# Two attribute maps in one product, and a shorter first piece of each layer's input, in a three-layer graph network on one Trainium2 core

## The chip, the cores and the metric

The kernel runs on one core of one Trainium2 chip. The metric is the device time of one execution in microseconds (us). The text calls the engines by the names that the profile uses: PE multiplies matrices (PEld is its loading of the stationary operand), DVE is the vector engine, ACT the scalar engine, POOL the general one, and SP issues transfers.

## The reference, cut to what matters

There are N = 6250 nodes with D = 64 features and E = 200000 edges with EC = 16 attributes; `src` and `dst` give the ends of an edge. A first network of two layers (SAGE) comes first and does not concern us. The second network has three message layers, each over the edges and one self loop for each node (whose attributes are all ones):

```
def _mp_layer(x, src_f, dst_f, ea_f, W, b):
    m = concatenate([x[dst_f], x[src_f], ea_f], axis=1) @ W.T + b
    return relu(segment_sum(m, dst_f, num_segments=n))

h = _mp_layer(x, ..., W0, b0);  h = relu(_batchnorm(h, g0, be0))
h = _mp_layer(h, ..., W1, b1);  h = relu(_batchnorm(h, g1, be1))
h = _mp_layer(h, ..., W2, b2)
x = layernorm(x + h)
```

Since a sum over edges and a linear map commute, a message layer is three sums per node: the adjacency matrix times the mapped features of the sources, the node's own mapped features times its in-degree, and the node's summed attributes (with its in-degree, for the bias) times the attribute part of W. The batch normalization takes mean and variance over all nodes, so no input of the next layer exists before the last node of a layer is done.

## The kernel before, in words

The nodes are padded to NB = 49 blocks of P = 128, in NT = 13 tiles of up to four blocks (TW = 512 nodes; the last tile has one block). A first half of the kernel builds the adjacency matrix as counts in 8 bits, `adj8`, tile by tile of destinations; every later layer loads a tile's 49 x 512 columns (`load_adj`) and multiplies. Features go in as three bf16 parts of 64 columns each, which together carry an fp32 value: `split` (L626 to L633) writes them into `parts`.

`ext` is a table of 128 rows by 6272 nodes. Its rows 0 to 47 are the three bf16 parts of the summed attributes, rows 48 to 63 are zero, and every row from 64 up holds the in-degree. `extT[n]` is the stationary side for layer n: the attribute columns of W three times, the bias at row 64, and zeros elsewhere.

`aggregate` (L640) makes the products of one or two tiles. `product` (L650) multiplies one 128 x 128 block of the adjacency with one block of `parts` (192 columns); 49 such products, one for each source block b, fill one destination block's sum in PSUM. `term` (L657) adds the node's attribute part to the same sum: one product of `ext` with `extT[n]` for each destination block, in layers 1 and 2 (`terms`). For the first two tiles of a layer (`src_first`), the loop over b is outside and the eight destination blocks inside, so that PE can start as soon as the first source block exists; `feed(b)` makes more source blocks on the way. For the other eleven tiles a destination block is the outer loop.

`next_input` (L1103) makes a piece of a layer's input from the layer before: ACT applies the normalization and the relu (L1107), PE multiplies with `maps` (L1110), `split` makes the three parts, and DVE makes the node's own share `own` (L1113, L1114). A piece has four blocks. `feed` calls it for piece 0 and piece 1 at b = 0 and for one piece more at every fourth block.

`first_message` (layer 0) sums the parts, transposes (L700, ACT copies the result to `mx`, L702), and makes two products into one PSUM tile `lin`: `catT` with the features (L1131) and `extT[0]` with `ext` (L1132). ACT takes the relu into `hr` (L1133). `message_layer` (layers 1 and 2) sums the parts (L675), adds `own` (L1142), and in layer 1 transposes (L1146) and takes the relu from PSUM into `hr` (L1147). `statistics` (L1118) collects a tile's mean and variance. At the end of a layer, L1188 to L1194 turn these into the scale and bias `sc`.

The order of instructions on each engine is made when the program is built, by a list scheduler that works from the program order and its own cost estimates. `pin` marks an instruction that is not to move against other marked ones. Pools decide how far an engine can run ahead: two `agg` tiles, two `u` tiles, one `tr` and one `lin` tile of PSUM, two buffers of `h1` (the input of L1110).

Of the kernel before, what the change touches and what calls it, by code (L numbers as in the profile page):

```python
# [11 lines left out]
F32 = mybir.dt.float32  # L12
# [4 lines left out]
AF = mybir.ActivationFunctionType  # L17
ALU = mybir.AluOpType
# [4 lines left out]
P = 128  # L23
# [453 lines left out]
def gnn_kernel(ctx: ExitStack, tc: tile.TileContext, x, src, dst, ea, W_l1, b_l1, W_r1, W_l2, b_l2, W_r2,  # L477
# [10 lines left out]
    nc = tc.nc  # L488
# [63 lines left out]
    with ExitStack() as fast:  # L552
# [22 lines left out]
        for n in range(3):  # L575


            if n == 0:
                catT.append(const.tile([2 * D, D], F32, name="catT"))
            else:  # L580
                maps.append(const.tile([D, 2 * D], F32, name=f"maps{n}"))
            extT.append(const.tile([P, D], F32, name=f"extT{n}"))
            nc.vector.memset(extT[n], 0.0)

        def load_weights():
            def transposed(to, of, at=0):
                p = psm.tile([P, P], F32, name="tr")
                k, m = of.shape
                nc.tensor.transpose(p[:m, :k], of, ident[:k, :k])
                nc.scalar.copy(to, p[:m, :k])  # L590

            nc.sync.dma_start(bl1, b_l1.rearrange("(p o) -> p o", o=1))
            nc.sync.dma_start(bl2, b_l2.rearrange("(o d) -> o d", o=1).to_broadcast([P, D]))
            for to, w in ((w1s[:D, :], W_l1), (w1s[D:, :], W_r1), (w2s[:, :D], W_l2), (w2s[:, D:], W_r2)):
                t = spare(w.shape[1])[: w.shape[0], :]
                nc.sync.dma_start(t, w)
                transposed(to, t)
            for n, (w, b) in enumerate(((W0, b0), (W1, b1), (W2, b2))):
                t = spare(2 * D + 3 * EC)[:D, :]
                for r in range(3):  # L600
                    nc.sync.dma_start(t[:, 2 * D + r * EC: 2 * D + (r + 1) * EC], w[:, 2 * D:])
                nc.sync.dma_start(t[:, : 2 * D], w[:, : 2 * D])
                nc.sync.dma_start(extT[n][D: D + 1, :], b.rearrange("(o d) -> o d", o=1))
                if n == 0:
                    transposed(catT[0], t[:, : 2 * D])
                else:
                    transposed(maps[n - 1][:, D:], t[:, : D])
                    transposed(maps[n - 1][:, : D], t[:, D: 2 * D])
                transposed(extT[n][: 3 * EC, :], t[:, 2 * D:])
            for n, (g, be) in enumerate(((g0, be0), (g1, be1))):  # L610
                gam.append(const.tile([D, 1], F32, name=f"gam{n}"))
                bet.append(const.tile([D, 1], F32, name=f"bet{n}"))
                nc.sync.dma_start(gam[n], g.rearrange("(p o) -> p o", o=1))
                nc.sync.dma_start(bet[n], be.rearrange("(p o) -> p o", o=1))
# [25 lines left out]
        def aggregate(psa, pt, tiles, n, src_first=False, feed=None, terms=None, sources=range(NB)):  # L640

            views = [view(a, j) for a, j in tiles]
            sums = [psa.tile([P, 4, TW // 2], F32, name="agg") for _ in tiles]
            blocks = [(k, i) for k, (_, j) in enumerate(tiles) for i in range(tw(j) // P)]

            def product(k, i, b):

                nc.tensor.matmul(sums[k][:, i, :n], views[k][:, b, i * P: (i + 1) * P], pt[:, b, :n],  # L650
                                 start=(b == sources[0] and terms is None and not (src_first and i % 2)), stop=(b == sources[-1]),
                                 skip_group_check=src_first or terms is not None)

            def term(k, i):
                if terms is not None:
                    at = tiles[k][1] * TW + i * P
                    nc.tensor.matmul(sums[k][:, i, : terms[1].shape[1]], terms[0][:, at: at + P], terms[1],  # L657
                                     start=not (src_first and i % 2), stop=False, skip_group_check=True)

            if src_first:  # L660
                for k, i in blocks:
                    term(k, i)
                for b in sources:
                    feed(b)
                    for k, i in blocks:
                        product(k, i, b)
            else:
                for k, i in blocks:
                    term(k, i)
                    for b in range(NB):  # L670
                        product(k, i, b)
            return sums
# [61 lines left out]
        with ExitStack() as bld:  # L734
# [315 lines left out]
            hot = bld.enter_context(tc.tile_pool(name="ahot", bufs=2))  # L1050
            lhss = [ew.tile([P, EAG, P], BF16, name=f"lhs{k}", bufs=1) for k in range(2)]
            for lhs in lhss:
                nc.gpsimd.memset(lhs[:, :, 3 * EC: D], 0.0)
                nc.gpsimd.memset(lhs[:, :, D:], 1.0)
            selfl = ew.tile([P, 1], F32, name="selfl", bufs=1)
            nc.vector.memset(selfl, 0.0)
            nc.vector.memset(selfl[:EC, :], 1.0)
            nc.vector.memset(selfl[D:, :], 1.0)


            per = -(-NSUB // NT)
# [32 lines left out]

        mp = fast.enter_context(tc.tile_pool(name="fmp", bufs=1))
        hr = mp.tile([D, NPAD], F32, name="hr")
        own = mp.tile([P, NB, D], F32, name="own")
        ok_s = mp.tile([1, 1], I32, name="ok_s")
        psu = fast.enter_context(tc.tile_pool(name="fpsu", bufs=2, space=PSUM))
        nc.sync.dma_start(ok_s, ok_d)  # L1100
        nc.vector.tensor_single_scalar(inv, cnt, 1.0, ALU.add)

        def next_input(n, b, sc, pt):  # L1103

            nb, s = min(4, NB - b), slice(b * P, min(b + 4, NB) * P)
            y = work.tile([D, TW], F32, name="h1")
            nc.scalar.activation(y[:, : nb * P], hr[:, s], AF.Relu, bias=sc[:, 1:2], scale=sc[:, 0:1])  # L1107
            u = psu.tile([P, 4, P], F32, name="u")
            for i in range(nb):
                nc.tensor.matmul(u[:, i, :], y[:, i * P: (i + 1) * P], maps[n - 1], start=True, stop=True)  # L1110
            split(pt[:, b: b + nb, : 3 * D], u[:, :nb, :D], nb)
            o = own[:, b: b + nb, :]
            nc.vector.tensor_mul(o, u[:, :nb, D:], inv[:, b: b + nb].unsqueeze(2).to_broadcast([P, nb, D]))  # L1113
            nc.vector.tensor_add(o, o, u[:, :nb, :D])  # L1114
# [5 lines left out]
        def first_message(j, ps, stats):  # L1120

            w, s = tw(j), slice(j * TW, j * TW + tw(j))
            nb, bs = w // P, j * TW // P
            h = res[:, bs: bs + nb, :]
            nd = work.tile([P, 4, P], F32, name="nd")
            nc.gpsimd.tensor_tensor(nd[:, :nb, :D], h, inv[:, bs: bs + nb].unsqueeze(2).to_broadcast([P, nb, D]), ALU.mult)  # L1126
            add_parts(nd[:, :nb, D:], ps, nb)
            nc.vector.tensor_add(nd[:, :nb, D:], nd[:, :nb, D:], h)
            both = transposed_tile(nd, nb)
            pm = psm.tile([P, TW], F32, name="lin")  # L1130
            nc.tensor.matmul(pm[:D, :w], catT[0], both[:, :w], start=True, stop=False)  # L1131
            nc.tensor.matmul(pm[:D, :w], extT[0], ext[:, s], start=False, stop=True)  # L1132
            nc.scalar.activation(hr[:, s], pm[:D, :w], AF.Relu)  # L1133
            statistics(j, stats)

        def message_layer(n, j, ps, stats):
# [6 lines left out]
            if n < 2:  # L1143
                t = psm.tile([P, 4, P], F32, name="tr")
                for i in range(nb):
                    nc.tensor.transpose(t[:D, i, :], v[:, i, :], ident)  # L1146
                nc.scalar.activation(hr[:, s], t[:D, :nb, :].rearrange("f i p -> f (i p)"), AF.Relu)  # L1147
                statistics(j, stats)
                return
            nc.vector.scalar_tensor_tensor(v[:, :nb, :], v[:, :nb, :], 0.0, res[:, bs: bs + nb, :], ALU.max, ALU.add)  # L1150
# [8 lines left out]
        sc = None  # L1159
        for n in range(3):  # L1160
            pt = parts[n % 2]
            terms = (ext, extT[n]) if n else None
            stats = work.tile([D, NT, nc.vector.BN_STATS_DIM], F32, name="stats") if n < 2 else None
            first = [(load_adj(j), j) for j in range(2)]

            def feed(b):
                if n and b % 4 == 0:
                    if b == 0:
                        next_input(n, 0, sc, pt)
                    if b + 4 < NB:  # L1170
                        next_input(n, b + 4, sc, pt)

            def message(j, ps):
                if n == 0:
# [11 lines left out]
                break  # L1186
            mv = work.tile([D, nc.vector.BN_AGGR_DIM], F32, name="mv")
            nc.vector.bn_aggr(mv, stats.rearrange("p j s -> p (j s)"))  # L1188
            sc = work.tile([D, 2], F32, name="sc")
            nc.scalar.activation(sc[:, 0:1], mv[:, 1:2], AF.Sqrt, bias=eps_t[:D])  # L1190
            nc.vector.reciprocal(sc[:, 0:1], sc[:, 0:1])
            nc.vector.tensor_mul(sc[:, 0:1], sc[:, 0:1], gam[n])
            nc.vector.tensor_mul(sc[:, 1:2], mv[:, 0:1], sc[:, 0:1])
            nc.vector.tensor_sub(sc[:, 1:2], bet[n], sc[:, 1:2])  # L1194
        ok_r = nc.values_load(ok_s[0:1, 0:1], min_val=0, max_val=1)

    with tc.If(ok_r == 0):
# [32 lines left out]
```

## Time and profile before

| | |
|---|---|
| median of 3 runs | 1657.76 us (1656.78 to 1659.83) |
| profiled execution: its own time | 1656.98 us |
| its span, first to last instruction | 1655.2 us |
| mean granted PE clock in it | 0.964 |
| build and first network, with the attribute sums (0 to 945 us of the span) | PE busy 810 us, DVE 767 us, ACT 511 us |
| message layer 0 (945 to 1170) | PE busy 220.7 us, DVE 31.1 us, ACT 13.8 us |
| message layer 1 (1170 to 1411.8) | PE busy 236.5 us, DVE 48.9 us, ACT 26.1 us |
| message layer 2 (1411.8 to the end) | PE busy 229.4 us, DVE 73.1 us, ACT 27.4 us |

The stages were cut at the ends of the layers' last adjacency products. The profile gives the busy time of an engine, what ended its idle times, and the chain of work that ended last; "issue" in that chain is time for which the profile shows no cause.

### The profile page before, as it was taken

How to read it: one execution, taken by the hardware profiler on the slowest of the kernel's cores; microseconds unless marked ns; L12 is line 12 of the kernel's file. 1: busy time of each engine (PE TensorE's matmuls, PEld its weight loads, DVE VectorE, ACT ScalarE, POOL GpSimd, SP SyncE). 2: the span in 40 equal slices, each digit the busy share in tenths (PEclk: the TensorE clock that was granted, in tenths of full speed). 3: DMA queues.
4: the chain of work that ended last, by engine and by line, in shares of the span. 5: the costliest groups of instructions: out<-in, count | busy, mean ns of one | idle time of the engine just before them, and what ended most of it. 6: DMA issues, size and time to landing. Idle time of an engine off the chain costs nothing.

```text
span 1655.2 us, 38577 instructions
## 1 busy us (share of the span) xinstructions
PE 1496.9 (90%) x17135; PEld 1379.9 (83%) x17135; DVE 920.0 (56%) x1581; ACT 578.4 (35%) x1088; POOL 117.0 (7%) x72
## 2 busy tenths in 40 slices
PE   1586789899998989999999999999999999999997
PEld 0475668788887779889999888888899999899997
DVE  2999999998898733897888610001340100442122
ACT  1625466776885721454455300000220000310000
POOL 2024200360001010000000000000000000000000
PEclk9697899999999999999999999999899999899999
DMA  5021332032130373344534444442324542345450
GB/s 163 11 107 55 110 96 85 12 154 83 80 157 2 150 287 159 137 150 183 200 133 142 172 165 179 187 173 99 156 117 197 197 194 99 157 178 227 164 186 10
DMA packets 43811, 228.10 MB, mean 138 GB/s; under 512 B 22978, under 2 KB 30210, under 8 KB 35826
## 3 DMA queue, kind: packets, MB, share of 16 engines
q1 hardware_dynamic: 37058, 139.54, 22.4%
q10 hardware_dynamic: 4496, 79.48, 12.2%
q0 software_dynamic: 2080, 6.52, 1.3%
q8 instruction: 136, 2.23, 0.5%
q14 instruction: 41, 0.34, 0.1%
HBM read 183.76 MB, written 41.75 MB: 136 GB/s over the span
## 4 chain that ended last, share of the span: by engine, by line
PE 62%; DVE 21%; ACT 7%; issue 5%; DMA 3%; ACTq 0%; POOL 0%; DVEq 0%; POOLq 0%
PE agg L650 47%; DVE lo L620 7%; PE pair L958 6%; DVE rhs L620 4%; ACT a L965 4%; PE u L1110 2%; PE bank L1025 2%; DVE e L1016 1%; PE agg L657 1%; DVE e L1018 1%; DMA e<-in_edge_attr_dram 1%; DVE nd L675 1%; PE tr L700 1%; PE lin L1131 1%; DMA a<-adj 1%
## 5 line engine op out<-in xcount | busy, mean ns | idle before, releaser
L650 PE MATMUL agg<-parts,a 128*128 128x192 bf16 (+1 forms) x12005 | 1089.8, 246 | 5.6 <-DVE nd L675 1.8
L650 PEld LDWEIGHTS <-a 128*128 128x128 fp8e3 x12005 | 1008.3, 98 | 23.6 <-issue 12.1
L965 ACT ACTIVATE a<-pair 128x784 fp8e3<-128x784 f32 (+3 forms) x355 | 292.3, 890 | 122.8 <-PE pair L958 121.2
L958 PE MATMUL pair<-rhs,lo 128*128 128x147 bf16 (+5 forms) x2569 | 266.2, 244 | 64.0 <-DVE lo L620 30.3
L958 PEld LDWEIGHTS <-lo 128*128 128x128 bf16 x2569 | 196.2, 104 | 119.4 <-issue 52.1
L620 DVE TENSOR_TENSOR rhs<-iota,k 128x1960 bf16<-128x1960 f16 (+15 forms) x240 | 238.9, 1015 | 13.6 <-ACT k L905 11.3
L620 DVE TENSOR_TENSOR lo<-iota,k 128x2048 bf16<-128x2048 f16 x161 | 194.5, 1215 | 0.0
L675 DVE TENSOR_REDUCE z<-agg 128x256 f32<-128x768 f32 (+1 forms) x39 | 35.3, 910 | 282.7 <-PE agg L650 282.4
L620 DVE TENSOR_TENSOR lo<-iota,e_d 128x2048 bf16<-128x2048 f16 (+11 forms) x132 | 130.7, 1010 | 20.6 <-PE bank L1025 19.8
L1025 PE MATMUL bank<-lo,lhs 128*128 128x128 bf16 x1701 | 107.5, 219 | 17.4 <-ACT lhs L1019 12.1
L1025 PEld LDWEIGHTS <-lhs 128*128 128x128 bf16 x1701 | 98.4, 98 | 28.6 <-ACT lhs L1019 19.4
L675 DVE TENSOR_REDUCE nd<-agg 128x256 f32<-128x768 f32 (+1 forms) x26 | 23.4, 904 | 116.0 <-PE agg L650 116.0
L886 POOL DMA_INDIRECT rows<-cmb_d,start_i x21 | 64.8, 3084 | 207.4 <-ACT key L897 167.0
L1118 DVE BATCH_NORM_STATS2 stats<-hr 64x6 f32<-64x512 f32 (+1 forms) x26 | 17.0, 653 | 101.7 <-ACT hr L1133 80.4
L702 ACT COPY mx<-tr 128x512 f32<-128x512 f32 (+1 forms) x26 | 14.6, 562 | 166.9 <-PE tr L700 166.8
L691 ACT ACTIVATE sp_r<-z 128x256 f32<-128x256 f32 (+1 forms) x26 | 10.5, 403 | 171.4 <-DVE z L690 171.4
L1147 ACT ACTIVATE hr<-tr 64x512 f32<-64x512 f32 (+1 forms) x13 | 7.4, 566 | 179.9 <-PE tr L1146 179.9
L1015 ACT CAST lhs<-e 128x512 bf16<-128x512 f32 (+21 forms) x72 | 36.1, 502 | 59.6 <-PE bank L1025 44.6
L1126 POOL TENSOR_TENSOR nd<-res,inv 128x256 f32<-128x256 f32 (+1 forms) x13 | 7.6, 589 | 550.5 <-DVE ln_s L688 339.2
L1019 ACT CAST lhs<-e 128x512 bf16<-128x512 f32 (+21 forms) x72 | 36.4, 505 | 23.1 <-DVE e L1018 22.6
L1016 DVE TENSOR_TENSOR e<-e,lhs 128x512 f32<-128x512 f32 (+21 forms) x72 | 39.4, 550 | 8.9 <-ACT lhs L1015 8.8
L1017 ACT CAST lhs<-e 128x512 bf16<-128x512 f32 (+21 forms) x72 | 36.3, 504 | 22.2 <-DVE e L1016 21.0
(140 smaller groups left out, 819.6 us busy)
## 6 DMA issues: line engine op xcount, KB each, us to landing
a<-adj SPq DMA_DIRECT2D x24, 3136.0 KB, 12.4
a<-adj ACTq DMA_DIRECT2D x24, 3136.0 KB, 11.5
adj<-a SPq DMA_DIRECT2D x12, 3136.0 KB, 9.6
e<-in_edge_attr_dram SPq DMA_DIRECT2D x25, 256.0 KB, 2.7
a<-adj SPq DMA_DIRECT2D x4, 784.0 KB, 4.2
out_dram<-z SPq DMA_DIRECT2D x12, 128.0 KB, 6.5
a<-first_edges ACTq DMA_DIRECT2D x1, 1216.0 KB
e<-in_edge_attr_dram SPq DMA_DIRECT2D x7, 152.0 KB, 3.3
```

Of the source, the lines that this page charges most:

```text
L620: nc.vector.tensor_tensor(to.rearrange("p g (h two) -> p g h two", two=2), iota[:, :n].rearrange("p (h two) -> p h two", two=2).unsqueeze( ...
L650: nc.tensor.matmul(sums[k][:, i, :n], views[k][:, b, i * P: (i + 1) * P], pt[:, b, :n], start=(b == sources[0] and terms is None and not ( ...
L675: nc.vector.tensor_reduce(to, ps[:, :nb, : 3 * D].rearrange("p b (r d) -> p b d r", r=3), AX.X, ALU.add)
L886: pin(nc.gpsimd.indirect_dma_start(out=rows, out_offset=None, in_=cmb_d[:, :], in_offset=bass.IndirectOffsetOnAxis(ap=start_i[:, t: t + 1] ...
L958: nc.tensor.matmul(pair[:, bank % 2, col: col + wc], lo_hot(t, c), rhs[:, i, :wc], start=first, stop=last)
L965: nc.scalar.activation(av[:, :, o: o + 2 * nd].rearrange("p h (two d) -> p h two d", two=2), pair[:, :, : nd * NB].rearrange("p two (d h) ...
L1015: nc.scalar.copy(lhs[:, :g, 0:EC], r)
L1016: nc.vector.tensor_sub(r, r, lhs[:, :g, 0:EC])
L1017: nc.scalar.copy(lhs[:, :g, EC:2 * EC], r)
L1019: nc.scalar.copy(lhs[:, :g, 2 * EC:3 * EC], r)
L1025: nc.tensor.matmul(ps[:, :P], lhs[:, q, :], oh[:, q % HOT, :], start=(c == 0 and q == 0), stop=(i == last_b[b] and q == g - 1))
L1110: nc.tensor.matmul(u[:, i, :], y[:, i * P: (i + 1) * P], maps[n - 1], start=True, stop=True)
```

## The change

Layer 1's attribute part is taken out of its sums. Instead the product that makes layer 0's attribute part makes layer 1's at the same time: `extT[0]` and `extT[1]` lie side by side in one 128-column stationary operand, `ext01`, and the upper 64 rows of the result are layer 1's share for these nodes. ACT copies them to `e1`, which is the upper half of `ext` itself, whose rows are not needed for these nodes after that. In layer 1, DVE adds `e1` to the transposed sums and ACT takes the relu in place. So that layer 2 finds all that it needs in the lower half of `ext`, the in-degree now begins at row 48, and the bias with it. In layer 0 the `ext` product comes ahead of the `catT` product in program order.

A layer's input now begins with a piece of one block and a piece of three; then come pieces of four as before, and the last of one. Layer 2's `term` products of the first two tiles stand behind the first two pieces in program order, no longer ahead of them, and these and the products of `next_input` are pinned. In the chain from statistics to `sc`, the mean's sign is turned first, and one operation with two steps takes the place of a multiplication and a subtraction.

```diff
-            extT.append(const.tile([P, D], F32, name=f"extT{n}"))
+            if n == 0:
+                ext01 = const.tile([P, 2 * D], F32, name="ext01")
+            extT.append(ext01[:, n * D: (n + 1) * D] if n < 2 else const.tile([P, D], F32, name="extT2"))
...
-                nc.sync.dma_start(extT[n][D: D + 1, :], b.rearrange("(o d) -> o d", o=1))
+                nc.sync.dma_start(extT[n][3 * EC: 3 * EC + 1, :], b.rearrange("(o d) -> o d", o=1))
...
             def term(k, i):
...
+                    if src_first:
+                        pin(first)
             if src_first:
-                for k, i in blocks:
-                    term(k, i)
                 for b in sources:
                     feed(b)
+                    if b == sources[0]:
+                        for k, i in blocks:
+                            term(k, i)
...
-                nc.gpsimd.memset(lhs[:, :, 3 * EC: D], 0.0)
-                nc.gpsimd.memset(lhs[:, :, D:], 1.0)
+                nc.gpsimd.memset(lhs[:, :, 3 * EC:], 1.0)
...
+        e1 = ext[D:, :]
...
-        def next_input(n, b, sc, pt):
+        def next_input(n, b, end, sc, pt):
-            nb, s = min(4, NB - b), slice(b * P, min(b + 4, NB) * P)
+            nb, s = end - b, slice(b * P, end * P)
...
-                nc.tensor.matmul(u[:, i, :], y[:, i * P: (i + 1) * P], maps[n - 1], start=True, stop=True)
+                pin(nc.tensor.matmul(u[:, i, :], y[:, i * P: (i + 1) * P], maps[n - 1], start=True, stop=True))
...
-            nc.tensor.matmul(pm[:D, :w], catT[0], both[:, :w], start=True, stop=False)
-            nc.tensor.matmul(pm[:D, :w], extT[0], ext[:, s], start=False, stop=True)
+            nc.tensor.matmul(pm[:, :w], ext01, ext[:, s], start=True, stop=False, skip_group_check=True)
+            nc.tensor.matmul(pm[:D, :w], catT[0], both[:, :w], start=False, stop=True, skip_group_check=True)
             nc.scalar.activation(hr[:, s], pm[:D, :w], AF.Relu)
+            nc.scalar.copy(e1[:, s], pm[D:, :w])
...
-                nc.scalar.activation(hr[:, s], t[:D, :nb, :].rearrange("f i p -> f (i p)"), AF.Relu)
+                nc.vector.tensor_add(hr[:, s], t[:D, :nb, :].rearrange("f i p -> f (i p)"), e1[:, s])
+                nc.scalar.activation(hr[:, s], hr[:, s], AF.Relu)
...
-            terms = (ext, extT[n]) if n else None
+            terms = (ext[:D, :], extT[n][:D, :]) if n == 2 else None
...
             def feed(b):
-                if n and b % 4 == 0:
-                    if b == 0:
-                        next_input(n, 0, sc, pt)
-                    if b + 4 < NB:
-                        next_input(n, b + 4, sc, pt)
+                ends = [1] + list(range(4, NB, 4)) + [NB]
+                if n and b == 0:
+                    next_input(n, 0, ends[0], sc, pt)
+                if n and b in [0] + ends[:-1]:
+                    q = ([0] + ends).index(b)
+                    if q + 1 < len(ends):
+                        next_input(n, ends[q], ends[q + 1], sc, pt)
...
+            nc.vector.tensor_single_scalar(mv[:, 0:1], mv[:, 0:1], -1.0, ALU.mult)
...
-            nc.vector.tensor_mul(sc[:, 1:2], mv[:, 0:1], sc[:, 0:1])
-            nc.vector.tensor_sub(sc[:, 1:2], bet[n], sc[:, 1:2])
+            nc.vector.scalar_tensor_tensor(sc[:, 1:2], sc[:, 0:1], mv[:, 0:1], bet[n], ALU.mult, ALU.add)
```

More of the change, by code (lines that the diff above doesn't have):

```diff
@@ L656, in term @@
                     at = tiles[k][1] * TW + i * P
-                    nc.tensor.matmul(sums[k][:, i, : terms[1].shape[1]], terms[0][:, at: at + P], terms[1],
-                                     start=not (src_first and i % 2), stop=False, skip_group_check=True)
+                    first = nc.tensor.matmul(sums[k][:, i, : terms[1].shape[1]], terms[0][:, at: at + P], terms[1],
+                                             start=not (src_first and i % 2), stop=False, skip_group_check=True)
+                    if src_first:
+                        pin(first)
             if src_first:
-                for k, i in blocks:
-                    term(k, i)
                 for b in sources:
                     feed(b)
+                    if b == sources[0]:
+                        for k, i in blocks:
+                            term(k, i)
                     for k, i in blocks:
@@ L1052, in gnn_kernel @@
             for lhs in lhss:
-                nc.gpsimd.memset(lhs[:, :, 3 * EC: D], 0.0)
-                nc.gpsimd.memset(lhs[:, :, D:], 1.0)
+                nc.gpsimd.memset(lhs[:, :, 3 * EC:], 1.0)
             selfl = ew.tile([P, 1], F32, name="selfl", bufs=1)
-            nc.vector.memset(selfl, 0.0)
+            nc.vector.memset(selfl, 1.0)
+            nc.vector.memset(selfl[:32, :], 0.0)
+            nc.vector.memset(selfl[32: 3 * EC, :], 0.0)
             nc.vector.memset(selfl[:EC, :], 1.0)
-            nc.vector.memset(selfl[D:, :], 1.0)
             per = -(-NSUB // NT)
```

## The prediction, made before the changed kernel ran

> **What bounds the kernel now.** I first read the page's shares: PE is busy for 1496.9 of 1655.2 us. The chain that ended last says where that matters. In the message layers it runs through PE almost without a break, so there a product removed is time won. This is the chain in the middle of layer 1 (start, duration, what):
>
> ```profile
> 1248.37 1.32 PE agg L650 x16
> 1249.69 0.08 issue
> 1249.78 0.60 PE tr L1146 x4
> 1250.37 2.72 PE agg L650 x33
> 1253.10 0.20 PE agg L657 x2
> 1253.29 4.04 PE agg L650 x49
> 1257.34 0.20 PE agg L657 x2
> 1257.53 4.04 PE agg L650 x49
> ```
>
> A destination block costs 4.04 us of adjacency products and 0.20 us for its attribute term (two passes). The transpose of a finished tile waits 0.08 us in each of the long tiles: `tr` starts 1.60 us after the tile's last product, for DVE has to sum and add first.
>
> Only between two layers does the chain leave PE. Here are the end of layer 1 and the beginning of layer 2:
>
> ```profile
> 1411.84 1.76 PE agg L657 x16
> 1413.60 0.12 PE tr L1146
> ...
> 1415.77 0.16 DVE sc L1194
> ...
> 1416.02 0.82 ACT h L1107
> 1416.84 0.04 issue
> 1416.88 3.79 PE u L1110 x16
> 1420.67 0.08 issue
> 1420.75 2.04 PE u L1110 x8
> ```
>
> Layer 2's eight terms (1.76 us) hold up the last transpose; then PE idles for 3.16 us until ACT has made the first piece; then come three pieces of `u` (5.91 us) before any adjacency product. The third view is the stretches of this boundary, with the granted clock third from the right (the stretches are chosen 3.41 us long; PE busy is the first number after the comma):
>
> ```profile
> 1412.60:1416.01 3.41, 1.11 (x10) 0.89 (x9) 1.86 (x7) 0.57 (x2) 0.00 (x0) 1.00 0.90 380
> 1416.01:1419.43 3.42, 2.55 (x12) 2.55 (x13) 0.03 (x1) 1.96 (x4) 0.00 (x0) 0.50 1.04 447
> 1419.43:1422.84 3.41, 3.32 (x15) 2.83 (x15) 3.16 (x10) 2.33 (x6) 0.00 (x0) 0.50 1.06 456
> 1422.84:1426.25 3.41, 3.41 (x23) 3.23 (x23) 2.04 (x7) 1.37 (x3) 0.00 (x0) 0.50 0.07 29
> 1426.25:1429.66 3.41, 3.41 (x44) 3.40 (x41) 0.00 (x0) 0.00 (x0) 0.00 (x0) 1.00 0.00 0
> ```
>
> After a stretch with PE a third busy, PE runs at half clock for three stretches: 23 products in the third, against 44 in the one after it. The second is full of `u` products, and still the clock does not come back; it comes back after the first stretch full of adjacency products. The boundary before (1177.08 to 1187.32) reads the same.
>
> [...] So 128 columns in `ext01` should cost little more than 64 (the trace has 0.14 us for a load of 64 columns and 0.19 for 128), and layer 2's terms gain nothing from having 64 rows in place of 128.
>
> **Part by part.** I read the order on PE from the built program of both versions; it shows more than the diff.
>
> *Layer 1's tiles.* 49 terms go. Eight stood at the boundary and are counted there; 41 x 0.20 = -8.2 us. But the transpose of a long tile now stands 17 products behind the tile's end instead of a term and 16: 17 x 0.0825 = 1.40 us, where its input needs 1.60. The wait grows from 0.08 to 0.20: 11 x 0.12 = +1.3. DVE's new addition (64x512 with PSUM; nearest rows: 0.42 us for 128x256, 0.69 for the statistics of 64x512, so about 0.65) lies beside PE: DVE is busy 49 of 242 us here, and the next `tr` is 196 products away. Behind the first two tiles only 10 products separate two transposes, 0.83 us, just enough. Without that cover it would cost 13 x 0.65. Sum **-6.9** (-8.2 to -5.5).
>
> *Layer 0's tiles.* The `ext` product now stands at the tile's end, ahead of the transpose and 8 products. Before, the transpose came after 17 products (1.40 us) and waited 0.25 for an input that takes 1.65; now 1.00 + 0.66 cover it: 11 x -0.25 = -2.75. But in the chain a lone product of the pair costs 1.00 us and the second of a pair 0.86: standing apart costs 12 x 0.14 = +1.7. ACT's copy into `e1` (0.57, nearest the relu's 0.59) is hidden: ACT is busy 14 of 225 us, and the next user of `lin` comes 8 or more products later. Sum **-1.0** (-2.7 to +1).
>
> *Boundary 0 to 1,* from the last adjacency product, T = 1170.03, to the end of the first 64 products, 1191.09: 21.06 us before. Now the terms (1.76) are gone; 0.87 of `ext` product are ahead of T and still count. `catT` takes 1.00; then ACT has three things in line (relu, the new copy, `mx`), so the last `catT` starts at about T+3.2 and ends at T+3.65 (before T+5.11). From there to `sc` took 2.21; one operation less makes 2.03 (the sign change hides beside ACT's root, 0.30 us): `sc` at S = T+5.7. The first ACT piece has 128 columns (0.49 by the last piece's row, against 0.82), so `u` starts at S+0.56 and its parts go through ACT and DVE in turn. ACT has a 512-column piece (0.8) between two steps, and DVE has the second piece's subtraction in line; I get the first adjacency product at S+3.75 (before, S+6.74). But it has only 8 products of food; then PE's order is four blocks of `u`, 24 products, four of `u`, 32 products. At half clock: 1.3 + 2.0 + 3.9 + 2.0 + 5.2 = 14.4, so T+23.9 if the clock never rose. [...] the first place for one is the run of 24, T+12.7 to 16.6, so it rises between T+15.1 and 17.6. From the middle, 16.4, the rest runs at 0.52 of its time: 16.4 + 0.52 x 7.5 = T+20.3. **-0.8** (-2 to +2).
>
> *Boundary 1 to 2,* T = 1411.84, before 17.97 us to the end of the 64 products. The terms no longer stand before the last transpose: it starts when DVE is done, T+0.76 instead of 1.76. The new addition is 0.23, and the statistics of tile 11 (0.68) now stand on DVE between it and the last ones, a further 0.43: S = T+3.6 (before 4.09). Then one and three blocks of `u`, done at S+2.7, and now the eight terms, at half clock: by `u`'s ratio (2.0 against 1.08) 3.3 us, so S+6.0; the gap that they fill would have lasted to S+3.75. The same 14.4 follow: T+24.0 without a rise. The run of 24 begins at T+12.9; the rise is at 15.3 to 17.8, middle 16.6; end 16.6 + 0.52 x 7.4 = T+20.4. **+2.5** (0 to +5).
>
> *At nothing:* layer 2's other tiles (same terms); the memsets, `selfl` and three bias rows to another partition, same number of SP transfers, two fewer on POOL: all at the beginning or under the attribute stage, where DVE's one-hots cover them; bare, they are under 1 us. No transfer is moved.
>
> Sum: -6.9 - 1.0 - 0.8 + 2.5 = -6.2 against the profiled execution's own 1656.98 us: 1650.8. The median is 0.8 above that execution, well inside the runs' 3 us[...]; I take **1651.0**.
>
> **The rivals.**
> 1. *The boundaries give what their idle time promises.* [...] 2 x 1.7 less, about 1647. Against it: the stretch 1419.43, busy 3.32 of 3.42, did not raise it.
> 2. *The run of 24 is too short.* Both boundaries then wait for the run of 32, some 3.4 us of half clock later, 1.7 each, and small stalls of `tr` on top: about 1654.5, the edge of what can be told from no change.
> 3. *Slower.* The clock stays at half while `u` and adjacency products alternate: a piece with its 32 products takes 7.2 us in place of the chain's 3.83, 3.4 lost each. From three pieces without a rise on (+10) the change loses: 1661. Against it: 32 products at half clock last 5.2 us[...].
> 4. *It does not do what it says*: layer 1 keeps its terms, or PE waits for `e1`. The built order shows no term in layer 1, and `e1` is written a whole layer earlier.
>
> **How the numbers follow.** About 0.2%, 3.3 us, can be told from no change: faster is below 1654.4. The forecast has 0.60, rival 1 0.15, rival 2 0.17 (half of it faster), a wider mishap at the boundaries or in layer 0 that ends within 0.2% 0.04, rival 3 0.03, rival 4 0.01. Faster: 0.60 + 0.15 + 0.09 + 0.03 = 0.87; same 0.09; slower 0.04. The range takes rival 1 and rival 2 in: 1646 to 1656.
>
> **What would show it.** Layer 1's chain should have blocks of 4.04 us with nothing between, and waits of 0.2 before `tr`. Boundary 1 to 2 should show the terms after `u`, near 3.3 us long, and more time from T to the end of the first 64 products than 17.97; the clock should come back in or after the run of 24. I am wrong if layer 1's tiles gain less than 5.5, if PE waits for ACT or DVE at every tile, or if the second boundary gains.

## The result: slower by about a third of a per cent

The changed kernel has a median of 1663.86 us (1660.32 to 1666.44, 8 runs), the kernel before 1657.49 us beside it (1656.64 to 1662.96, 8 runs). The ratio is 1.0034, with a 95% interval of 1.002 to 1.0047: some 5.6 us slower by the ratio (the medians lie 6.4 apart). Forecast were 1651 us and a range of 1646 to 1656.

The profiled execution took 1666.44 us, its span is 1664.7; it lies 2.6 us above its median, where that of before lay 0.5 below. So its span shows 9.5 us of difference, and not all of that belongs to the change. The chain that ended last, cut at the same places in both, says where they are (us from the start of the span). Its last product of layer 2 is that of the twelfth tile; behind it the chain runs through DVE, and the one block of the thirteenth tile lies beside that.

| | before | after | this part |
|---|---|---|---|
| last product of layer 0 | 1170.03 | 1171.49 | +1.46 (+2.17 before the layer, -0.71 in it) |
| first 64 products of layer 1 done | 1191.09 | 1191.89 | -0.66 |
| last product of layer 1 | 1411.84 | 1405.87 | -6.77 |
| first 64 products of layer 2 done | 1429.88 | 1427.52 | +3.61 |
| last product of layer 2 in the chain | 1640.87 | 1649.21 | **+10.70** |
| end of the span | 1655.2 | 1664.7 | +1.16 |

The 2.17 us ahead of layer 0 and the 1.16 at the end cannot be put down to the change: layer 0 ends between 1166.4 and 1175.3 us in the ten profiles of this study, and at the end of the span the last store landed 0.8 us later behind its issue and DVE waited 0.4 us for the store before it. In between, everything up to the last product of layer 1 came out near the forecast sums. The loss is in layer 2's long tiles, which had been put at nothing. The chain of after in the middle of layer 2 (start, duration, what):

```profile
1512.30 0.36 PE agg L659 x2
1512.66 4.20 PE agg L652 x49
1516.86 0.36 PE agg L659 x2
1517.22 4.20 PE agg L652 x49
```

The same stretch of the kernel before:

```profile
1512.11 0.20 PE agg L657 x2
1512.30 4.09 PE agg L650 x49
1516.40 0.20 PE agg L657 x2
1516.59 4.09 PE agg L650 x49
```

A destination block takes 4.56 us instead of 4.29. The term costs 0.16 more, and 0.11 more lies in the 49 products behind it. The stretch of the table has 40 such terms: 40 x 0.27 = 10.8 us. The 41st, of the thirteenth tile, lies beside DVE's work. The loads of stationary operands alone, in the timeline, show how. After first, then before (start, duration, engine, line, operation, rows*columns and shape, count, in brackets the idle time ahead of it):

```profile
1521.35 0.29 PEld L659 LDWEIGHTS agg<-extT,ext 64*128 64x128 f32 x2 [0.16 <-issue]
1521.71 4.04 PEld L652 LDWEIGHTS <-a 128*128 128x128 fp8e3 x49
```

```profile
1524.74 0.30 PEld L657 LDWEIGHTS agg<-extT,ext 128*128 128x128 f32 x2
1524.90 4.14 PEld L650 LDWEIGHTS <-a 128*128 128x128 fp8e3 x49
```

Before, one load follows on the other without a gap. With 64 rows the loader stands idle for 0.16 us ahead of the term, and the load of the next product begins only 0.36 us after the term's first one, where before it began after 0.16. In the same timelines the term's load starts 0.08 us ahead of its first product in before (1524.74 and 1524.82), and the load behind the terms 0.11 us ahead of its own (1524.90 and 1525.01); in after it is 0.00 us (both 1521.35) and 0.01 us (1521.71 and 1521.72). So both loads have lost their lead on their products, and the chain is longer by 0.16 and 0.11 us at these two places.

Layer 1's tiles without terms look as they were meant to. Each transpose still waits for DVE's two operations, of which all but 0.2 us is covered by adjacency products:

```profile
1248.34 0.02 issue
1248.36 0.97 DVE z L680
1249.33 0.02 issue
1249.35 0.43 DVE z L1149
1249.79 0.14 issue
1249.92 0.60 PE tr L1153 x4
1250.52 14.78 PE agg L652 x179
```

And this is the second boundary, where the terms now stand behind the pieces:

```profile
1410.86 1.64 PE u L1116 x6
1412.51 3.31 PE agg L659 x16
1415.81 1.40 PE agg L652 x8
1417.20 2.01 PE u L1116 x8
1419.21 3.96 PE agg L652 x24
1423.17 1.60 PE u L1116 x8
```

### The profile page after: what moved, and what is told of

Its sections match the earlier page's. It is cut to its first block, busy times and chain, and to the rows that moved or that the text cites. A ratio compares the mean times of both kernels' runs of the same rounds, so it can differ in the third digit from the quotient of the medians.

```text
span 1664.7 us, 38428 instructions
## 1 busy us (share of the span) xinstructions
PE 1505.2 (90%) x17037; PEld 1375.8 (83%) x17037; DVE 930.6 (56%) x1605; ACT 587.3 (35%) x1107; POOL 85.6 (5%) x70
## 4 chain that ended last, share of the span: by engine, by line
PE 62%; DVE 22%; ACT 7%; issue 5%; DMA 3%; ACTq 0%; POOL 0%; DVEq 0%; POOLq 0%
PE agg L652 47%; DVE lo L622 8%; PE pair L963 6%; DVE rhs L622 5%; ACT a L970 4%; PE u L1116 2%; PE bank L1030 2%; DVE z L680 1%; DVE e L1021 1%; DVE e L1023 1%; PE agg L659 1%; PE lin L1138 1%; PE tr L705 1%; DMA a<-adj 1%; PE lin L1137 1%
## 5 line engine op out<-in xcount | busy, mean ns | idle before, releaser
L622 DVE TENSOR_TENSOR lo<-iota,e_d 128x2048 bf16<-128x2048 f16 (+11 forms) x132 | 130.8, 1011 | 20.5 <-PE bank L1030 19.9
L1030 PE MATMUL bank<-lo,lhs 128*128 128x128 bf16 x1701 | 107.5, 219 | 16.4 <-ACT lhs L1024 11.0
L1030 PEld LDWEIGHTS <-lhs 128*128 128x128 bf16 x1701 | 98.4, 98 | 27.5 <-ACT lhs L1024 18.3
L1155 ACT ACTIVATE hr<-hr 64x512 f32<-64x512 f32 (+1 forms) x13 | 7.9, 605 | 172.2 <-DVE hr L1154 172.2
L891 POOL DMA_INDIRECT rows<-cmb_d,start_i x21 | 33.5, 1594 | 241.0 <-ACT key L902 199.4
L1021 DVE TENSOR_TENSOR e<-e,lhs 128x512 f32<-128x512 f32 (+21 forms) x72 | 39.4, 551 | 8.0 <-ACT lhs L1020 7.9
L1023 DVE TENSOR_TENSOR e<-e,lhs 128x512 f32<-128x512 f32 (+21 forms) x72 | 39.3, 547 | 7.3 <-ACT lhs L1022 6.7
```

The source lines that it names most:

```text
L622: nc.vector.tensor_tensor(to.rearrange("p g (h two) -> p g h two", two=2), iota[:, :n].rearrange("p (h two) -> p h two", two=2).unsqueeze( ...
L891: pin(nc.gpsimd.indirect_dma_start(out=rows, out_offset=None, in_=cmb_d[:, :], in_offset=bass.IndirectOffsetOnAxis(ap=start_i[:, t: t + 1] ...
L1021: nc.vector.tensor_sub(r, r, lhs[:, :g, 0:EC])
L1023: nc.vector.tensor_sub(r, r, lhs[:, :g, EC:2 * EC])
L1030: nc.tensor.matmul(ps[:, :P], lhs[:, q, :], oh[:, q % HOT, :], start=(c == 0 and q == 0), stop=(i == last_b[b] and q == g - 1))
```

## The experiments

Theory A is my reading of these loads: the price, 0.16 us at the term and 0.11 us behind it, is that of the switch of the row count, which a lone 64-row term among 128-row products pays for twice. Theory B puts the price on the 64-row product itself. Theory C looks elsewhere in layer 2. Each version was timed beside the kernel before on the same chip, so ratios are compared, not medians of different sessions.

**128 rows for layer 2's terms.** The upper half of the table now holds layer 1's shares; the weights are zero there.

```diff
-            terms = (ext[:D, :], extT[n][:D, :]) if n == 2 else None
+            terms = (ext, extT[n]) if n == 2 else None
```

> The changed kernel, but layer 2's terms again with all 128 rows of the table (the upper rows now hold layer 1's share, against zeros in the weights). Theory A (a product with 64 rows between products with 128 rows cannot have its operand loaded ahead, and neither can the one after it: 0.27 us for each lone term): the pitch of a destination block in layer 2 falls from 4.56 to 4.29 us, 41 x 0.27 = 11 us less, so about 1653 us, faster than before by some 4.5. Theory B (each 64-row term is itself slower by 0.27 us, whatever stands beside it): the same. Theory C (layer 2 is slower for another reason, such as the upper half of the table being written): pitch stays 4.56, 1664 us.

Measured: 1654.31 us beside 1659.02, ratio 0.9969 (0.996 to 0.9977). The chain has the old pitch again:

```profile
1505.87 0.20 PE agg L659 x2
1506.06 4.10 PE agg L652 x49
1510.16 0.20 PE agg L659 x2
1510.36 4.09 PE agg L652 x49
```

This one line takes back 0.65% of the time, 10.8 us, and turns the change from a loss into a gain. Theory C is out; A and B both allow this.

**64 rows, but four terms together.**

```diff
                 for k, i in blocks:
                     term(k, i)
+                for k, i in blocks:
                     for b in range(NB):
                         product(k, i, b)
```

The products are pinned behind them, and of each two destination blocks only the first one's term starts the sum.

> The changed kernel with its 64-row terms, but in layer 2's long tiles the four terms of a tile stand together ahead of the tile's 196 products, so the row count switches 11 times instead of 41. Theory A: 30 x 0.27 = 8 us less than the changed kernel, about 1656 us. Theory B: no difference, 1664 us.

Measured: 1658.66 us beside 1659.02, ratio 0.9997 (0.9985 to 1.0008), against 1.0034 for the changed kernel: 6 us less, with the same number of the same 64-row products. Theory B allows none of that. The chain shows a whole tile, and the loader's timeline the terms of the same tile with one idle time ahead of all eight passes:

```profile
1513.56 1.03 PE agg L661 x8
1514.59 16.49 PE agg L652 x196
1531.08 1.03 PE agg L661 x8
```

```profile
1513.48 0.96 PEld L661 LDWEIGHTS agg<-extT,ext 64*128 64x128 f32 x8 [0.16 <-issue]
```

Eight passes take 1.03 us. Two alone take 0.36, so the six others take 0.11 each, about the 0.10 of a pass with 128 rows (0.20 for two). A tile takes 17.52 us, against 4 x 4.56 = 18.24 with the terms apart and 4 x 4.29 = 17.16 with 128 rows: two thirds of the loss is gone, ten tiles give 7.2 us, a little less than the 8 expected, for a group costs 0.36 and not 0.27. Of these two theories the runs bear out A: the cost followed the switches, not the number of products with 64 rows.

**64-row terms in the kernel before, nothing else** (with the in-degree and the bias from row 48).

```diff
-            terms = (ext, extT[n]) if n else None
+            terms = (ext[:D, :], extT[n][:D, :]) if n else None
```

> The kernel before with one part alone: the in-degree begins at row 48, and the terms of layers 1 and 2 use 64 rows. Nothing else is changed. Theories A and B: 82 lone terms x 0.27 = 22 us slower than before, about 1679 us, with a pitch of 4.56 instead of 4.29 in both layers. Theory C: within 2 us of before, 1657 us.

Measured: 1678.96 us beside 1659.02, ratio 1.013 (1.0114 to 1.0145): 21.6 us slower by the ratio, 19.9 by the medians, where 82 x 0.27 = 22.1. Here is the chain in layer 2, then around a transpose in layer 1:

```profile
1500.51 0.36 PE agg L657 x2
1500.87 4.20 PE agg L650 x49
```

```profile
1267.03 0.36 PE agg L657 x2
1267.39 1.43 PE agg L650 x16
1268.82 0.44 PE tr L1146 x4
```

In the profile layer 2's 41 terms cost 11.0 us and layer 1's 41 terms 8.5. Layer 1's blocks are 0.27 longer as well, but the longer term covers the wait ahead of each transpose: its 0.08 is gone, and four transposes take 0.44 where they took 0.60. The cost needs nothing else of the change.

**128 rows, and layer 2's first terms ahead of the pieces again.**

```diff
+                for k, i in blocks:
+                    term(k, i)
                 for b in sources:
                     feed(b)
-                    if b == sources[0]:
-                        for k, i in blocks:
-                            term(k, i)
```

> As the 128-row version, and layer 2's first eight terms stand ahead of the pieces again, as in the kernel before, and are not pinned. If the boundary between layers 1 and 2 lost its 3.7 us because the terms run at half clock after the pieces, it gives some 2 to 3.5 us back: end of layer 1 to the end of the first 64 products falls from 21.65 to 18 to 19.5 us, total about 1650. If the loss comes from the short first piece (8 products, then four blocks of u before more), it stays above 21 and the total at 1653.

Measured: 1653.43 us beside 1659.02, ratio 0.9964 (0.9952 to 0.9976). For the rest of the experiments the boundaries are compared in the profiles: from the last product of a layer to the first `u` product behind the first 64 products of the next, read in the timeline.

| | 0 to 1 | 1 to 2 |
|---|---|---|
| before | 20.99 | 17.97 |
| changed kernel | 20.33 | 21.58 |
| 128 rows | 19.72 | 21.11 |
| 128 rows, terms ahead | 20.15 | 18.38 |
| the same, pieces of four | 19.99 | 18.51 |
| joint product alone | 19.60 | 18.35 |
| terms ahead, PE kept busy | 16.08 | 14.81 |
| the same, pieces of four | 16.52 | 15.46 |

The second boundary is 2.7 us shorter with the terms ahead, as expected, but the total fell by under 1 us between the two versions, and the intervals overlap: the step is seen in one profile of each and not in the times. In the same profile another limit comes up. The chain leads to PE through the load of the second tile's adjacency:

```profile
1402.94 0.02 issue
1402.96 12.92 DMA a<-adj
1415.88 0.05 issue
1415.93 0.82 PE agg L652 x4
```

In the program this load waits until the last but one tile of the layer before gives its buffer back; it was issued at 1402.96. The last product here was at 1407.76 and the load landed 8.1 us behind it, so in this run no product of the second tile could come earlier, however soon the first piece is made. The wait itself is short: the four products of the first tile ran from 1415.04 on.

**The same with pieces of four.**

```diff
-                ends = [1] + list(range(4, NB, 4)) + [NB]
+                ends = list(range(4, NB, 4)) + [NB]
```

> The version with 128 rows and terms ahead, with pieces of four again from the beginning (products of the pieces still pinned: two pieces, then 32 products). If the short first piece is worth what the earlier first adjacency product suggests (3 us at each boundary), this is some 4 to 6 us slower than with pieces of one and three, 1657 to 1659. If it is worth nothing, because half clock and the load of the second tile's adjacency set the end of the first 64 products, the two are within 1.5 us, about 1653.

Measured: 1651.07 us beside 1660.54, ratio 0.9939 (0.9926 to 0.9952). The boundaries differ by 0.16 and 0.13 us in the two profiles, with opposite signs. The short first piece brings nothing here. In times, the version with pieces of four has the lower ratio, but the two were timed in different sessions; that one and three cost something is not settled.

**The joint product alone, in the kernel before** (with the copy into `e1` and DVE's addition; 128 rows, terms in their old place, pieces of four, the old chain to `sc`).

```diff
-            nc.tensor.matmul(pm[:D, :w], catT[0], both[:, :w], start=True, stop=False)
-            nc.tensor.matmul(pm[:D, :w], extT[0], ext[:, s], start=False, stop=True)
+            nc.tensor.matmul(pm[:, :w], ext01, ext[:, s], start=True, stop=False, skip_group_check=True)
+            nc.tensor.matmul(pm[:D, :w], catT[0], both[:, :w], start=False, stop=True, skip_group_check=True)
...
-            terms = (ext, extT[n]) if n else None
+            terms = (ext, extT[n]) if n == 2 else None
```

> The kernel before with the joint product alone: layer 1's share from layer 0's product, degree from row 48 on, layer 2's terms with all 128 rows and in their old place, pieces of four, the old chain to sc. If the joint product is what carries the gain: layer 1's tiles 6.8 less, layer 0's tiles and the first boundary about 1 less, so 7 to 8 us faster than before, about 1651 beside 1659. If the short first piece and the new order carry part of it, it stays slower than the version with 128 rows and terms ahead (1653), at 1655 or more.

Measured: 1651.19 us beside 1660.54, ratio 0.9944 (0.9931 to 0.9957), 9.3 us faster than before. The joint product carries the gain; the other parts of the change add nothing that these runs can tell.

**PE kept busy at the boundaries** (terms ahead, one and three). Products without a use are put in, old parts with old parts into a free PSUM tile; their results go nowhere, and the last transpose and the last `catT` product are pinned ahead of them.

```diff
                 if n and b == 0:
+                    busy(26)
                     next_input(n, 0, ends[0], sc, pt)
...
+                if n and b == 0:
+                    busy(10)
```

> The version with 128 rows and terms ahead, pieces of one and three, and at each of the two boundaries 26 products without a use (old parts with old parts, into a free PSUM tile) ahead of the first piece and 10 behind the second, so that PE does not stand idle. If half clock is what the boundaries lose, the granted clock stays at 1.0 there and each boundary gets 3 to 4 us shorter: 7 us less, about 1646. If the clock is not the cause or goes down all the same: 1653 to 1656.

Measured: 1644.67 us beside 1660.54, ratio 0.9905 (0.989 to 0.992), 15.8 us faster than before and the fastest version of the study. Here are stretches of the second boundary (length, PE busy first after the comma, granted clock third from the right):

```profile
1402.70:1406.10 3.40, 3.40 (x39) 3.40 (x38) 2.37 (x7) 0.50 (x2) 0.00 (x0) 1.00 0.89 384
1406.10:1409.50 3.40, 2.49 (x22) 1.95 (x21) 1.48 (x9) 2.68 (x8) 0.00 (x0) 1.00 1.10 472
1409.50:1412.90 3.40, 3.40 (x38) 3.12 (x36) 2.30 (x8) 1.99 (x5) 0.00 (x0) 1.00 1.03 440
1412.90:1416.30 3.40, 3.40 (x38) 3.12 (x36) 2.02 (x6) 1.57 (x4) 0.00 (x0) 1.00 0.39 157
```

The version without these products (128 rows, terms ahead) has half clock for 10.24 us at the same boundary, from 1411.65 to 1421.89. Two of its stretches:

```profile
1411.65:1415.07 3.42, 2.27 (x9) 1.91 (x10) 1.21 (x6) 2.42 (x7) 0.00 (x0) 0.50 0.96 411
1418.48:1421.89 3.41, 3.41 (x23) 3.05 (x22) 1.80 (x5) 1.38 (x3) 0.00 (x0) 0.50 0.28 120
```

With the products the clock stays at 1.0 through both boundaries. `sc` and the first piece come no sooner: the first `u` product starts 5.81 us (first boundary) and 4.76 us (second) behind the layer's last product, against 5.81 and 4.75 without. Each boundary is 3.6 to 4.1 us shorter all the same. So half clock costs these 3.6 to 4.1 of the 18 to 20 us.

**The same with pieces of four.**

```diff
-                ends = [1] + list(range(4, NB, 4)) + [NB]
+                ends = list(range(4, NB, 4)) + [NB]
```

> The same products without a use, with pieces of four. At full clock the short first piece should show what it is worth: if the parts of the first piece set the first adjacency product, this is 1 to 2 us slower at each boundary than with one and three, about 1649; if the load of the second tile's adjacency sets it (about 9 us after the layer's last product), the two are within 1.5 us.

Measured: 1648.05 us beside 1660.54, ratio 0.9916 (0.9897 to 0.9935). At full clock the first piece of one block is worth 0.44 and 0.65 us in the profiles, less than the 1 to 2 us of the first reading and within what the second one allows. The intervals of the two ratios overlap widely, so the times do not tell them apart.

## Why the prediction was wrong

*The step that failed* is the line "At nothing: layer 2's other tiles (same terms)", and ahead of it "layer 2's terms gain nothing from having 64 rows in place of 128". They gain nothing, but I took that for costing nothing: I priced the row count by the duration of the load and the product, and not by what it does to the products on both sides. The term of the sum was 0; it measured 10.70 us in the profile (40 x 0.27 = 10.8), and the version with 128 rows took 10.8 us back. My sum of -6.2 with 10.7 added is +4.5; measured are some +5.6 by the ratio.

That price did not show in the duration of a load: two took 0.29 us with 64 rows and 0.30 with 128. It came from the moment when the load begins, and there the row count mattered: 0.16 us of idle loader ahead of each lone term, and 0.11 us more in the products behind it. Why the loader stands idle there was not shown; shown is that the cost goes with the number of switches (10.8 us for 40 lone terms, 10 x 0.36 = 3.6 for the same terms in ten groups).

The trace of before held the warning. Its `u` products have 64 rows and stand among 128-row products; in its timeline their loads have 0.16 us of idle time ahead, though ACT had made their input at least 5 us earlier, while the loads of the 128-row terms have none:

```profile
1191.02 0.96 PEld L1110 LDWEIGHTS u<-maps,h 64*128 64x128 f32 x8 [0.16 <-issue]
```

The view alone does not prove it: loads of the 128-row transposes have idle time ahead as well (0.28 us at 1249.75), where they wait for DVE, whose addition ran from 1249.20 for 0.42 us.

*Layer 1's tiles* were right: -6.9 forecast, -6.77 measured for all between the first 64 products and the last, with the longer wait ahead of the transposes (0.20 against 0.08 in each of ten tiles, 2.0 us in all against 0.8).

*Layer 0's tiles* came out near the sum, -1.0 forecast and -0.71 measured, but by luck: both of its terms were too large and of opposite sign. The wait ahead of a transpose fell from 0.25 to 0.11 us and not to nothing (ten tiles: -1.4, not -2.75). Standing apart cost 0.03 a tile and not 0.14 (0.89 and 1.00 us for the two products, against 1.86 for the pair: +0.4, not +1.7).

*Boundary 0 to 1* was right, -0.8 forecast and -0.66 measured, with two small misses that cancel: `sc` came 5.2 us after the last product (5.7), and the clock rose at T+17.2. My times for the rise (middle 16.4, latest 17.6) were an estimate; the view of before showed only that it came after the first stretch full of adjacency products. The first adjacency product started 5.5 us earlier than before, and the end of the 64 moved by 0.66 only: up to there PE had the same twelve blocks of `u` and 64 products to do, and half clock lasted until T+17.2, as before (T+17.3).

*Boundary 1 to 2* was right in kind and a little small: +2.5 forecast, +3.6 measured, inside its bounds. `sc` came 3.8 us after the last product (3.6), the terms took 3.31 us at half clock (3.3), the first adjacency product started 6.2 us after `sc` (6.0). The clock came back at about T+18.3, half a microsecond later than my latest time, which was an estimate too. Stretches with a mean clock of 0.69 (1409.28 to 1412.70) and 0.81 (1422.9 to 1426.3) put the fall at 1410.6 and the rise at 1424.2, if the clock was at 1.00 before and behind and at 0.50 between, as in the stretches around them: 13.6 us apart, where before it was 10.24 (1416.01 to 1426.25). The stretch from 1417.4 to 1420.8 reached into the run of 24 but held 1.8 us of `u` products, and the clock in it was 0.50. With the terms ahead, the boundary is back at 18.4.

*The rivals:* the clock did not stay down through the pieces (rival 3, my case for a slower kernel; it rose at T+17.2 and T+18.3), and the terms did leave layer 1 (rival 4). Rival 2 came in small: at the second boundary the clock rose later than I allowed, but before the run of 32. Rival 1 did not happen; in its place the run with busy products shows that the gain it named exists, if PE is given products like the adjacency's (128 rows, 192 bf16 columns): 3.6 to 4.1 us at each boundary. No rival named the row count: all of them sat in the boundaries, and none asked what a narrower product does to its neighbours in a loop that runs 41 times.

## What to carry to other kernels

Before making a product narrower in rows, look in the trace of before for any product of that row count among others, and read the idle time of the weight loader ahead of it (0.16 us here) and the time of the products behind it (0.11 us more here); multiply by the number of switches, not of products. If rows are free, pad with zero weights, or put all the narrow products together. This is shown here for 64 rows among 128; other row counts were not tried. An edit whose work "stays the same" in count and shape of output can still change the form of an instruction in the longest loop of the kernel, and that is the first thing to price.

## What was not expected of the hardware

A lone 64-row product of two passes among 128-row products costs 0.27 us more than the same with 128 rows (4.56 against 4.29 us for a block), and four of them together cost 0.36 us more, not 1.08 (17.52 against 17.16 us for a tile). Having 128 rows was not enough to bring the clock back: in the version with 128 rows the 16 passes of the 128-row fp32 terms fill the second boundary from 1409.11 to 1412.71, and the stretch behind them is still at half clock (0.50). Whether the type or the 64 moving columns matter was not tested.

```profile
1409.29:1412.71 3.42, 3.42 (x18) 3.41 (x19) 1.63 (x5) 1.13 (x3) 0.00 (x0) 0.50 1.04 447
1412.71:1416.12 3.41, 3.41 (x19) 2.83 (x17) 0.00 (x0) 0.09 (x1) 0.00 (x0) 0.50 0.41 172
```

In before, a stretch of PE busy for 97% (3.32 of 3.42 us, from 1419.43), most of it with 64-row fp32 products, did not bring the clock back either: the next one was still at 0.50. With the 26 and 10 wide products the clock was 1.00 over the whole boundary, though one stretch of it had PE busy for only 2.49 of 3.40 us.
